# Convolution and involution in shared rounds of the array, and products in pairs (layer 1)

## The chip, the cores and the metric

The kernel runs on one core of a Trainium2 chip. The metric is the device time of one execution in microseconds. A profiled execution gives the trace, in which each engine's instructions stand with their start and length.

## What is computed

The program has two layers over 16 images of 16 channels and 256 x 256 points, all in float32. Layer 0 is a Laplace-type neural operator built on Fourier transforms; the change does not touch it. Layer 1 is this (cut to what matters; `x` is the group-normalised input, seen as B*C single-channel images):

```python
f = mish(conv2d(xs, W1, b1))                      # 1 -> 4 features, 3x3
top, bot = f[:, :, :H2], f[:, :, H2:]             # upper and lower half of the rows
ker = conv2d(relu(conv2d(bot, Wred, bred)), Wspan, bspan)   # 4 -> 1 -> 9, 1x1
patches = conv_general_dilated_patches(top, (3, 3), ...)    # 9 neighbours of each point
top_inv = (patches * ker[:, None]).sum(axis=2)    # the involution
shuffled = concatenate([ti, roll(bo, -1, axis=1)], axis=3).reshape(B, 4 * C, H, W)
out = mish(conv2d(shuffled, W2, b2))              # second convolution, 64 -> 16, 3x3
gate = sigmoid(...out.mean(axis=(2, 3))...)
return x * gate
```

Since `ker` is linear in the reduced value r with a bias per neighbour, the kernel forms the involution as (patches . Wspan) * r + (patches . bspan): two products on TensorE with fixed weights (`kernel` 0 and 1), a multiplication and an addition on VectorE.

## The kernel before

Layer 1 (function `layer1`) works in units. A unit is two places of one image, a place being 14 rows of each half and 8 of the 16 channels; an image has 9 units, so there are 144. Unit i's input `z` is loaded from the DRAM tensor `zn` two units ahead by SP's queue (`load_rows`, line 1115). Its steps on TensorE are these.

- `convolve(turn)`, line 1144, is the first convolution, half of the channel pairs in each of two turns. A product takes 18 rows of `z` (16 and the two neighbours) to 64 outputs, over 512 columns (2 channels x 256), and three products, one for each dx, add up in PSUM. The row group is given by half and place (4 groups of 32 rows), the column group by place and by `a`. So one round, dx fixed, is 8 products on 8 tiles of 32 x 64: the whole array of 128 x 128. The four PSUM banks are evacuated by Mish on ScalarE, into `bot` (line 1153) and into `feat`, which is one of the two `wide` tiles (line 1161).
- `reduce`, line 1172, makes r from `bot`: 8 products on tiles of 64 x 32, and a Relu on ScalarE. It then issues the stores of `bot` to the DRAM tensor `cf` from GpSimd's queue (line 1242).
- `involution(kernel)`, line 1194, takes 32 rows of `feat` to 32 outputs: one round, dx fixed, is 16 products on 16 tiles of 32 x 32. Its four banks `pd` are evacuated by VectorE: for kernel 0 `t = pd * r` (line 1209), for kernel 1 `top = pd + t` (line 1211). Then the eight stores of `top` to `cf` are issued (line 1224).
- The second convolution of the image before, `conv2`, runs beside the units of this one, one of its eight steps a unit. Its input `rows` comes back from `cf` (line 1250), VectorE makes four `planes` of sums and differences of it (line 1263), and TensorE forms four products (line 1272), each of 8 products of 128 x 32 on 4 tiles. VectorE and ScalarE combine them into the even and odd columns. The last image has a routine of its own, `conv2_last`.

All PSUM tiles of layer 1 come from one pool of eight banks (`bank`), which go round. The order of work on TensorE, ScalarE, VectorE and GpSimd is the order of the program (`tc.manual_schedule`), written out in the loop at the end of `layer1`. `conv2`, `gate` and `conv2_last` are generators; each `next` runs one to its next `yield`. With `nxt` the unit after `now`, TensorE's order in a usual unit is: convolve 0 of `nxt`, involution 0 of `now`, product 1, involution 1, product 2, convolve 1 of `nxt`, product 0, reduction of `nxt`, product 3. The ninth unit of an image, and all of the first image's, have no products.

Of the kernel before, what the change touches and what calls it, by code (L numbers as in the profile page):

```python
# [10 lines left out]
F32 = mybir.dt.float32  # L11
I32 = mybir.dt.int32
AF = mybir.ActivationFunctionType
ALU = mybir.AluOpType
# [5 lines left out]
N = 256  # L20
G = 8
P = 128
# [1001 lines left out]
def layer1(ctx, tc, d, zn, cf, mr, nb):  # L1024
# [17 lines left out]
    def bank(shape, name):  # L1042
        return banks.tile([P, *shape], F32, tag="bank", name=name)
# [76 lines left out]
    class Unit:  # L1120
# [3 lines left out]
        def __init__(self, b, i, n):  # L1124
            self.b, self.i = b, i
            j, h = divmod(n, 2)
            self.places = [(2 * j + s, 8 * h) for s in range(2)] if n < 8 else [(8, 0), (8, 8)]
            self.z = load_rows(b, self.places)

        def convolve(self, turn):  # L1130

            if turn == 0:
                self.bot = fp.tile([P, 8, 2, H], F32, tag="bot", name="bot")
                self.feat = wide[self.i % 2]
            ps = {(half, a): bank([2, N], "c1") for half in (1, 0) for a in range(2)}
            for dx in range(3):
                for a in range(2):
                    c = 4 * a + 2 * turn
                    for half in (1, 0):
                        for s in range(2):  # L1140
                            p = 32 * (2 * half + s)
                            lanes = slice(p, p + 18)
                            to = 64 * (s ^ a)
                            nc.tensor.matmul(  # L1144
                                ps[half, a][to : to + 64],
                                lhsT=w1[lanes, dx],
                                rhs=self.z[lanes, c : c + 2, dx : dx + N],
                                start=dx == 0,
                                stop=dx == 2,
                            )  # L1150
            for a in range(2):
                c = 4 * a + 2 * turn
                nc.scalar.activation(  # L1153
                    self.bot[:, c : c + 2],
                    ps[1, a].rearrange("p c (x e) -> p c e x", e=2)[:, :, ::-1],
                    AF.Mish,
                    bias=b1[1],
                )
            for a in range(2):
                c = 4 * a + 2 * turn  # L1160
                nc.scalar.activation(  # L1161
                    self.feat[:, c : c + 2, 1 : N + 1], ps[0, a], AF.Mish, bias=b1[0]
                )

        def reduce(self):

# [15 lines left out]
                nc.scalar.activation(self.r[:, s], ps[s], AF.Relu, bias=bred)  # L1182
            store_bot(self.b, self.places, self.bot)

        def involution(self, kernel):

            parts = [(s, fp_) for s in range(2) for fp_ in range(2)]
            ps = [bank([2, N], "pd") for _ in parts]
            for dx in range(3):
                for k in range(4):  # L1190
                    for (s, half), out in zip(parts, ps):
                        p = 64 * (s ^ k // 2) + 32 * half
                        lanes = slice(p, p + 32)
                        nc.tensor.matmul(  # L1194
                            out[32 * k : 32 * k + 32],
                            lhsT=dw[lanes, kernel, dx],
                            rhs=self.feat[lanes, 2 * k : 2 * k + 2, dx : dx + N],
                            start=dx == 0,
                            stop=dx == 2,
                        )  # L1200
            if kernel == 0:
                self.t = rp.tile([P, 2, 2, 2, 2, H], F32, tag="t", name="t", bufs=1)
                self.top = fp.tile([P, 2, 2, 2, 2, H], F32, tag="top", name="top")
            r = self.r.rearrange("p s (c q) x -> p s c q x", q=2)
            for (s, half), out in zip(parts, ps):
                out = out.rearrange("p c (x e) -> p c e x", e=2)[:, :, ::-1]
                t = self.t[:, s, half]
                if kernel == 0:
                    nc.vector.tensor_tensor(t, out, r[:, s], ALU.mult)  # L1209
                else:  # L1210
                    nc.vector.tensor_tensor(self.top[:, s, half], out, t, ALU.add)  # L1211
            if kernel:
                store_top(self.b, self.places, self.top)

    def valid(t):
        return (0 if t == 0 else 1), (16 if t == 8 else 15)
# [48 lines left out]
    def conv2(b, s, acc):  # L1265

        def products(terms):
            ps = bank([4, H], "c2ps")
            for i, (w, src) in enumerate(terms):
                for blk in range(2):  # L1270
                    for j in range(4):
                        nc.tensor.matmul(  # L1272
                            ps[32 * j : 32 * j + 32],
                            lhsT=w[:, blk],
                            rhs=src[:, 4 * j + blk : 4 * j + blk + 4],
                            start=(i, blk) == (0, 0),
                            stop=(i, blk) == (len(terms) - 1, 1),
                        )
# [12 lines left out]

        if b == nb - 1:
            yield from conv2_last(b, s, products, pooled)
            return
        a = rp.tile([P, 4, H], F32, tag="mid", name="mid", bufs=2)
        nc.scalar.copy(a, product(1))
        following(1)
        yield
        ps = product(2)
        even = rp.tile([P, 4, H], F32, tag="even", name="even", bufs=2)  # L1300
        odd = rp.tile([P, 4, H], F32, tag="odd", name="odd", bufs=2)
        yield
        nc.vector.tensor_tensor(even, ps, a, ALU.add)
        nc.vector.tensor_tensor(odd, a, ps, ALU.subtract)
        following(2)
        yield
        nc.vector.tensor_tensor(even, product(0), even, ALU.add)
        following(0)
        yield
        pooled(even, 0)  # L1310
        nc.vector.tensor_tensor(odd, odd, product(3), ALU.subtract)
        following(3)
        yield
        pooled(odd, 1)
        yield
# [80 lines left out]
    with tc.manual_schedule(engines={E.PE, E.Activation, E.DVE, E.Pool}):  # L1396
        begin_unit(0)
        begin_unit(1)
        u = units[0]
        u.convolve(0)  # L1400
        u.convolve(1)
        u.reduce()
        acc, last, first, second = None, iter(()), iter(()), iter(())
        for i in range(9 * nb + 12):
            b, s = divmod(i, 9)
            now, nxt = units.pop(i, None), units.get(i + 1)
            begin_unit(i + 2)
            if s >= 7 and b < nb:
                conv2_rows(b, s - 7)
            if b == nb and 0 < s < 7:  # L1410
                conv2_rows(b - 1, s + 1)
            if s < 6 and 0 < b < nb:
                conv2_rows(b - 1, s + 2)
            fresh = s == 8 and b < nb - 1
            gated = s == 8 and 0 < b <= nb
            next(last, None)
            if nxt:
                nxt.convolve(0)
            if s < 8 and b and b <= nb:
                if s == 0:  # L1420
                    acc = sm.tile([P, 16], F32, tag="acc", name="acc")
                second = conv2(b - 1, s, acc)
            if now:
                now.involution(0)
            next(first, None)
            next(second, None)
            if now:
                now.involution(1)
            if fresh:
                plane(b, 0, 1)  # L1430
            next(second, None)
            if gated:
                last = gate(b - 1, acc)
                next(last)
            if nxt:
                nxt.convolve(1)
            next(second, None)
            if fresh:
                plane(b, 0, 2)
            next(second, None)  # L1440
            if fresh:
                plane(b, 0, 0)
            if nxt:
                nxt.reduce()
            next(second, None)
            if gated:
                next(last)
            if fresh:
                plane(b, 0, 3)
            if gated:  # L1450
                next(last)
            next(last, None)
            first, second = second, iter(())

# [188 lines left out]
```

## Time and profile before

| | us |
|---|---|
| median of 3 runs (lowest, highest) | 5987.47 (5984.29, 5995.61) |
| profiled execution, its own time | 6010.53 |
| its span, from the first to the last instruction | 6008.8 |
| layer 1 within the span | from 2937 to 5975 |
| busy time of TensorE, VectorE, GpSimd, ScalarE over the span | 5572.9, 4666.5, 2802.4, 2310.8 |
| mean granted TensorE clock | 0.978 |

Busy times of one engine are the union of its instructions' times. The ends of matmuls are modelled, so TensorE's stages are measured from start to start. A float32 product leaves two MATMUL and two LDWEIGHTS records in the trace: 27648 records for the involution are 13824 products.

### The profile page before, as it was taken

Reading aid. Unit: us, or ns where it says so; the run is one execution under the profiler, and the core shown is the slowest. Engines: PE = TensorE matmul, PEld = TensorE weight load, DVE = VectorE, ACT = ScalarE, POOL = GpSimd, SP = SyncE. Lnnn points to the kernel's source line nnn. Section 1 sums busy time; section 2 is a strip of 40 time slices with the busy share of each in tenths; the row PEclk is TensorE's granted clock in tenths of the full one; section 3 lists DMA queues with packets and bytes.
Section 4 is the critical chain, followed back from the end, with each engine's and each line's share of the span. In section 5 each row is a group of like instructions: output and inputs, shape, how many; then the busy total and the mean of one; then the engine's idle time right before and its main releaser. Section 6 shows DMA issues by size and latency. Waiting matters only on the chain.

```text
span 6008.8 us, 216283 instructions
## 1 busy us (share of the span) xinstructions
PE 5572.9 (93%) x94280; PEld 3166.7 (53%) x94280; DVE 4666.5 (78%) x8643; ACT 2310.8 (38%) x4158; POOL 2802.4 (47%) x4090
## 2 busy tenths in 40 slices
PE   6999999688988888999899999999999999999996
PEld 5888888576766766777433333333333333333332
DVE  8888888388887876888557787777877778777784
ACT  2344556344444442222233333333333333333331
POOL 1344444333333335666544555544555445544453
PEclk9999999899999999999899999999999999999998
DMA  3455555566565658999677888888888888888886
GB/s 96 142 141 160 164 143 144 159 189 199 193 200 190 194 193 294 326 327 326 216 217 217 280 269 268 251 242 272 271 267 251 243 268 279 264 250 251 262 278 225
DMA packets 814469, 1370.07 MB, mean 228 GB/s; under 512 B 139824, under 2 KB 629168, under 8 KB 798384
## 3 DMA queue, kind: packets, MB, share of 16 engines
q1 hardware_dynamic: 596176, 881.61, 46.5%
q0 software_dynamic: 217344, 474.61, 25.8%
q8 instruction: 741, 12.14, 0.8%
q14 instruction: 208, 1.70, 0.1%
HBM read 729.78 MB, written 556.47 MB: 214 GB/s over the span
## 4 chain that ended last, share of the span: by engine, by line
PE 66%; DVE 20%; DMA 8%; issue 4%; ACT 1%; POOL 1%; SPq 1%; DVEq 0%; ACTq 0%; POOLq 0%
PE pd L1194 16%; PE c2ps L1272 15%; PE c L1144 12%; DMA z<-in_x 5%; PE ph L760 4%; PE ps L706 3%; PE pg L725 3%; PE pr L1172 2%; DVE planes L1263 2%; PE py L951 2%; PE py L952 2%; DVE st L167 2%; PE pt L741 2%; DVE zb L983 1%; DVE st L968 1%
## 5 line engine op out<-in xcount | busy, mean ns | idle before, releaser
L1224 POOL DMA_DIRECT2D cf<-top x1152 | 668.3, 692 | 1162.8 <-DVE top L1211 987.0
L1263 DVE TENSOR_TENSOR planes<-rows 128x1152 f32<-128x1152 f32 x960 | 1203.4, 1295 | 0.1
L1194 PE MATMUL pd<-wide,dw 32*32 32x512 f32 x27648 | 1032.8, 599 | 32.8 <-issue 17.6
L1153 ACT ACTIVATE bot<-c,b 128x512 f32<-128x512 f32 x576 | 364.8, 684 | 1450.9 <-PE c L1144 1099.4
L1144 PE MATMUL c<-z,w 18*64 18x512 f32 x13824 | 835.1, 601 | 15.7 <-DMA z<-zn 15.7
L1194 PEld LDWEIGHTS pd<-wide,dw 32*32 32x32 f32 x27648 | 446.6, 103 | 595.7 <-issue 455.5
L1209 DVE TENSOR_TENSOR t<-pd,r 128x512 f32<-128x512 f32 x576 | 357.5, 682 | 482.3 <-PE pd L1194 481.7
L1144 PEld LDWEIGHTS c<-z,w 18*64 18x64 f32 x13824 | 293.2, 132 | 533.4 <-issue 410.8
L1242 POOL DMA_DIRECT2D cf<-bot x720 | 395.4, 622 | 198.3 <-DMA cf<-top 81.2
L780 POOL TENSOR_TENSOR h<-w 128x256 f32<-128x256 f32 x258 | 211.4, 820 | 583.7 <-DVE w L774 580.8
L1272 PE MATMUL c2ps<-planes,c 128*32 128x512 f32 x3968 | 477.1, 598 | 0.0
L1211 DVE TENSOR_TENSOR top<-pd,t 128x512 f32<-128x512 f32 x576 | 357.4, 682 | 106.4 <-PE pd L1194 106.1
L1369 POOL TENSOR_SCALAR o<-o,scale,mean 128x258 f32<-128x258 f32 x488 | 355.5, 736 | 155.9 <-DVE scale L1361 141.5
L964 POOL TENSOR_TENSOR x<-x,o 128x512 f32<-128x512 f32 x256 | 324.5, 1268 | 215.1 <-DVE o L963 215.1
L205 PE MATMUL pu<-fy,f 128*128 128x128 f32 x2048 | 414.8, 285 | 1.1 <-ACT u L219 1.0
L212 PE MATMUL pv<-at,f 128*128 128x128 f32 x2048 | 403.1, 279 | 0.0
L322 POOL DMA_DIRECT2D al<-o x544 | 338.3, 629 | 118.1 <-ACT o L313 79.2
L1161 ACT ACTIVATE wide<-c,b 128x512 f32<-128x512 f32 x576 | 365.0, 693 | 0.0
L725 PE MATMUL pg<-alb,s 128*32 128x64 f32 x16896 | 288.0, 222 | 70.7 <-issue 52.3
L706 PE MATMUL ps<-tt,lt 64*32 64x256 f32 x8448 | 292.3, 388 | 54.0 <-issue 20.5
L951 PE MATMUL py<-h,iy 128*128 128x256 f32 x1024 | 316.4, 391 | 10.7 <-DMA h<-hd 10.7
L760 PE MATMUL ph<-ix,yt 64*128 64x128 f32 x4128 | 294.2, 281 | 31.2 <-DVE w L774 22.0
(244 smaller groups left out, 9937.8 us busy)
## 6 DMA issues: line engine op xcount, KB each, us to landing
rows<-cf SPq DMA_DIRECT2D x128, 2176.0 KB
cf<-top POOLq DMA_DIRECT2D x896, 112.0 KB, 5.5
cf<-bot POOLq DMA_DIRECT2D x336, 224.0 KB, 6.4
z<-zn SPq DMA_DIRECT2D x576, 129.0 KB
alb<-alx SPq DMA_DIRECT2D x132, 512.0 KB
zn<-zb SPq DMA_DIRECT2D x128, 516.0 KB
o<-zn SPq DMA_DIRECT2D x128, 516.0 KB
z<-in_x SPq DMA_DIRECT2D x64, 1024.0 KB
```

The source lines that it names most:

```text
L205: nc.tensor.matmul(pu[:, h, :, :, e].rearrange("p v g m -> p (v g) m"), lhsT=f[:, e, c, h], rhs=fy[:, e].rearrange("p (n m) -> p n m", m=2 ...
L212: nc.tensor.matmul(pv[:, a, h], lhsT=f[:, e, c, h], rhs=at[:, e, 4 * cg + c].rearrange("p l m -> p (l m)"), start=e == 0, stop=e == 1,)
L706: nc.tensor.matmul(ps[32 * g : 32 * g + 32, odd, v], lhsT=lt[lanes, kk, g, 1 - v : 3 - v].rearrange("p l c -> p (l c)"), rhs=tt[lanes, kk, g],
L725: nc.tensor.matmul(ps[32 * q : 32 * q + 32, x], lhsT=s[:, i].rearrange("p v k -> p (v k)"), rhs=alb[:, :, column(i)], start=True, stop=True,)
L760: nc.tensor.matmul(ph[q][:, e, blocks], lhsT=yt[lanes, i].rearrange("p t k -> p (t k)"), rhs=ix[lanes, i].rearrange("p (b x) -> p b x", b= ...
L951: nc.tensor.matmul(py[:, e], lhsT=iy[:, e], rhs=h[:, e, k % 4], start=True, stop=False)
L1144: nc.tensor.matmul(ps[half, a][to : to + 64], lhsT=w1[lanes, dx], rhs=self.z[lanes, c : c + 2, dx : dx + N], start=dx == 0, stop=dx == 2,)
L1194: nc.tensor.matmul(out[32 * k : 32 * k + 32], lhsT=dw[lanes, kernel, dx], rhs=self.feat[lanes, 2 * k : 2 * k + 2, dx : dx + N], start=dx == 0,
L1224: nc.gpsimd.dma_start(out=rows[y + 2 * lo : y + 2 * hi, :, c + 2 * k : c + 2 * k + 2].rearrange("y f c x -> y f (c x)"), in_=o[32 * k + 2 ...
L1242: nc.gpsimd.dma_start(out=rows[y + 4 * lo : y + 4 * hi, to : to + n].rearrange("p c x -> p (c x)"), in_=src.rearrange("p c q x -> p (c q x)"),
L1263: nc.vector.tensor_tensor(planes[:, k, rows], x[:, rows], y[:, rows], op_)
L1272: nc.tensor.matmul(ps[32 * j : 32 * j + 32], lhsT=w[:, blk], rhs=src[:, 4 * j + blk : 4 * j + blk + 4], start=(i, blk) == (0, 0), stop=(i, ...
```

## The change

`convolve` and `involution` no longer run as stages of their own. A new function `phases(nxt, now, turn)` takes both: for two groups y it opens two banks for the convolution and two for the involution, and for each dx it issues four convolution products (tiles of 32 x 64) and then eight involution products (tiles of 32 x 32) on the other eight sub-arrays. From y = 0 to y = 1 the two swap places. Evacuation becomes `activate` and `combine`, called after each group. A unit calls `phases` twice, with turn 0 and 1, which is also the involution's `kernel`. Two `yield`s leave `conv2` between products 1 and 2, and between 0 and 3. TensorE's order in a usual unit becomes: `phases` 0, products 1 and 2, `phases` 1, products 0 and 3, reduction. The stores of `top` are issued after `phases` 1.

The diff, without unchanged bodies:

```diff
@@ -1126,41 +1126,70 @@
...
             self.z = load_rows(b, self.places)
-
-        def convolve(self, turn):
-
-            if turn == 0:
+            self.feat = wide[i % 2]
+
+        def convolve(self, turn, banks_, dx):
+
+            for (half, a), ps in banks_.items():
+                c = 4 * a + 2 * turn
+                for s in range(2):
+                    p, to = 32 * (2 * half + s), 64 * (s ^ a)
+                    lanes = slice(p, p + 18)
+                    nc.tensor.matmul(
+                        ps[to : to + 64],
+                        lhsT=w1[lanes, dx],
+                        rhs=self.z[lanes, c : c + 2, dx : dx + N],
+                        start=dx == 0,
+                        stop=dx == 2,
+                    )
+
+        def activate(self, turn, banks_):
+
+            if turn == 0 and not hasattr(self, "bot"):
                 self.bot = fp.tile([P, 8, 2, H], F32, tag="bot", name="bot")
-                self.feat = wide[self.i % 2]
-            ps = {(half, a): bank([2, N], "c1") for half in (1, 0) for a in range(2)}
-            for dx in range(3):
-                for a in range(2):
-                    c = 4 * a + 2 * turn
-                    for half in (1, 0):
-                        for s in range(2):
-                            p = 32 * (2 * half + s)
-                            lanes = slice(p, p + 18)
-                            to = 64 * (s ^ a)
-                            nc.tensor.matmul(
-                                ps[half, a][to : to + 64],
-                                lhsT=w1[lanes, dx],
-                                rhs=self.z[lanes, c : c + 2, dx : dx + N],
-                                start=dx == 0,
-                                stop=dx == 2,
-                            )
-            for a in range(2):
+            for (half, a), ps in sorted(banks_.items(), reverse=True):
                 c = 4 * a + 2 * turn
...
-                )
+                if half:
+                    nc.scalar.activation(
+                        self.bot[:, c : c + 2],
+                        ps.rearrange("p c (x e) -> p c e x", e=2)[:, :, ::-1],
+                        AF.Mish,
+                        bias=b1[1],
+                    )
+                else:
+                    nc.scalar.activation(
+                        self.feat[:, c : c + 2, 1 : N + 1], ps, AF.Mish, bias=b1[0]
+                    )
+
+        def involution(self, kernel, banks_, dx):
+
+            for q in range(2):
+                for right in range(2):
+                    for (s, half), ps in banks_.items():
+                        k = 2 * right + q
+                        p = 64 * (s ^ right) + 32 * half
+                        lanes = slice(p, p + 32)
+                        nc.tensor.matmul(
+                            ps[32 * k : 32 * k + 32],
+                            lhsT=dw[lanes, kernel, dx],
+                            rhs=self.feat[lanes, 2 * k : 2 * k + 2, dx : dx + N],
+                            start=dx == 0,
+                            stop=dx == 2,
+                        )
+
+        def combine(self, kernel, banks_):
+
+            if kernel == 0 and not hasattr(self, "t"):
+                self.t = rp.tile([P, 2, 2, 2, 2, H], F32, tag="t", name="t", bufs=1)
+                self.top = fp.tile([P, 2, 2, 2, 2, H], F32, tag="top", name="top")
+            r = self.r.rearrange("p s (c q) x -> p s c q x", q=2)
+            for (s, half), ps in banks_.items():
+                ps = ps.rearrange("p c (x e) -> p c e x", e=2)[:, :, ::-1]
+                t = self.t[:, s, half]
+                if kernel == 0:
+                    nc.vector.tensor_tensor(t, ps, r[:, s], ALU.mult)
+                else:
+                    nc.vector.tensor_tensor(self.top[:, s, half], ps, t, ALU.add)
 
...
 
-        def involution(self, kernel):
-
-            parts = [(s, fp_) for s in range(2) for fp_ in range(2)]
-            ps = [bank([2, N], "pd") for _ in parts]
+    def phases(nxt, now, turn):
+
+        for y in range(2):
+            ours, theirs = ((0, y), (1, 1 - y)), ((1 - y, 0), (y, 1))
+            c1 = {part: bank([2, N], "c1") for part in ours if nxt}
+            pd = {part: bank([2, N], "pd") for part in theirs if now}
             for dx in range(3):
-                for k in range(4):
-                    for (s, half), out in zip(parts, ps):
-                        p = 64 * (s ^ k // 2) + 32 * half
-                        lanes = slice(p, p + 32)
-                        nc.tensor.matmul(
-                            out[32 * k : 32 * k + 32],
-                            lhsT=dw[lanes, kernel, dx],
-                            rhs=self.feat[lanes, 2 * k : 2 * k + 2, dx : dx + N],
-                            start=dx == 0,
-                            stop=dx == 2,
-                        )
...
-            if kernel:
-                store_top(self.b, self.places, self.top)
+                if nxt:
+                    nxt.convolve(turn, c1, dx)
+                if now:
+                    now.involution(turn, pd, dx)
+            if nxt:
+                nxt.activate(turn, c1)
+            if now:
+                now.combine(turn, pd)
+        if now and turn:
+            store_top(now.b, now.places, now.top)
...
@@ -1295,18 +1312,15 @@
...
         following(1)
-        yield
         ps = product(2)
         even = rp.tile([P, 4, H], F32, tag="even", name="even", bufs=2)
         odd = rp.tile([P, 4, H], F32, tag="odd", name="odd", bufs=2)
-        yield
         nc.vector.tensor_tensor(even, ps, a, ALU.add)
         nc.vector.tensor_tensor(odd, a, ps, ALU.subtract)
         following(2)
         yield
         nc.vector.tensor_tensor(even, product(0), even, ALU.add)
         following(0)
-        yield
         pooled(even, 0)
         nc.vector.tensor_tensor(odd, odd, product(3), ALU.subtract)
         following(3)
@@ -1396,14 +1410,13 @@
     with tc.manual_schedule(engines={E.PE, E.Activation, E.DVE, E.Pool}):
         begin_unit(0)
         begin_unit(1)
-        u = units[0]
-        u.convolve(0)
-        u.convolve(1)
-        u.reduce()
-        acc, last, first, second = None, iter(()), iter(()), iter(())
+        for turn in range(2):
+            phases(units[0], None, turn)
+        units[0].reduce()
+        acc, last, before = None, iter(()), iter(())
         for i in range(9 * nb + 12):
             b, s = divmod(i, 9)
-            now, nxt = units.pop(i, None), units.get(i + 1)
+            now, nxt, conv = units.pop(i, None), units.get(i + 1), iter(())
...
             fresh = s == 8 and b < nb - 1
             gated = s == 8 and 0 < b <= nb
             next(last, None)
-            if nxt:
-                nxt.convolve(0)
+            next(before, None)
+            phases(nxt, now, 0)
             if s < 8 and b and b <= nb:
                 if s == 0:
                     acc = sm.tile([P, 16], F32, tag="acc", name="acc")
-                second = conv2(b - 1, s, acc)
-            if now:
-                now.involution(0)
-            next(first, None)
-            next(second, None)
-            if now:
-                now.involution(1)
+                conv = conv2(b - 1, s, acc)
+            next(conv, None)
             if fresh:
                 plane(b, 0, 1)
-            next(second, None)
             if gated:
                 last = gate(b - 1, acc)
                 next(last)
-            if nxt:
-                nxt.convolve(1)
-            next(second, None)
             if fresh:
                 plane(b, 0, 2)
-            next(second, None)
+            phases(nxt, now, 1)
+            next(conv, None)
             if fresh:
                 plane(b, 0, 0)
             if nxt:
                 nxt.reduce()
-            next(second, None)
             if gated:
...
-            first, second = second, iter(())
+            before = conv
```

More of the change, by code (lines that the diff above doesn't have):

```diff
@@ L1128, in __init__ @@
             self.z = load_rows(b, self.places)
-        def convolve(self, turn):
-            if turn == 0:
-                self.bot = fp.tile([P, 8, 2, H], F32, tag="bot", name="bot")
-                self.feat = wide[self.i % 2]
-            ps = {(half, a): bank([2, N], "c1") for half in (1, 0) for a in range(2)}
-            for dx in range(3):
-                for a in range(2):
-                    c = 4 * a + 2 * turn
-                    for half in (1, 0):
-                        for s in range(2):
-                            p = 32 * (2 * half + s)
-                            lanes = slice(p, p + 18)
-                            to = 64 * (s ^ a)
-                            nc.tensor.matmul(
-                                ps[half, a][to : to + 64],
-                                lhsT=w1[lanes, dx],
-                                rhs=self.z[lanes, c : c + 2, dx : dx + N],
-                                start=dx == 0,
-                                stop=dx == 2,
-                            )
-            for a in range(2):
-                c = 4 * a + 2 * turn
[L1153 to L1157, printed above, removed]
-                )
[L1159 to L1162, printed above, removed]
-                )
@@ L1183, in reduce @@
             store_bot(self.b, self.places, self.bot)
-        def involution(self, kernel):
-            parts = [(s, fp_) for s in range(2) for fp_ in range(2)]
-            ps = [bank([2, N], "pd") for _ in parts]
-            for dx in range(3):
-                for k in range(4):
-                    for (s, half), out in zip(parts, ps):
-                        p = 64 * (s ^ k // 2) + 32 * half
-                        lanes = slice(p, p + 32)
-                        nc.tensor.matmul(
-                            out[32 * k : 32 * k + 32],
-                            lhsT=dw[lanes, kernel, dx],
-                            rhs=self.feat[lanes, 2 * k : 2 * k + 2, dx : dx + N],
-                            start=dx == 0,
-                            stop=dx == 2,
[L1200 to L1211, printed above, removed]
-            if kernel:
-                store_top(self.b, self.places, self.top)
+    def phases(nxt, now, turn):
[3 more added lines that the diff above has]
+            pd = {part: bank([2, N], "pd") for part in theirs if now}
+            for dx in range(3):
+                if nxt:
[8 more added lines that the diff above has]
+            store_top(now.b, now.places, now.top)
     def valid(t):
```

## Prediction

> **What bounds the kernel now.** The page is read first: where TensorE is busy, and what ended last.
>
> ```profile
> span 6008.8 us, 216283 instructions
> ...
> PE 5572.9 (93%) x94280; PEld 3166.7 (53%) x94280; DVE 4666.5 (78%) x8643; ACT 2310.8 (38%) x4158; POOL 2802.4 (47%) x4090
> ...
> PE 66%; DVE 20%; DMA 8%; issue 4%; ACT 1%; POOL 1%; SPq 1%; DVEq 0%; ACTq 0%; POOLq 0%
> PE pd L1194 16%; PE c2ps L1272 15%; PE c L1144 12%; DMA z<-in_x 5%; PE ph L760 4%; PE ps L706 3%; PE pg L725 3%; PE pr L1172 2%; DVE planes L1263 2%; PE py L951 2%; PE py L952 2%; DVE st L167 2%; PE pt L741 2%; DVE zb L983 1%; DVE st L968 1%
> ```
>
> The chain that ended last lies on TensorE, and its three longest lines (involution, second convolution, first convolution) are those that the change regroups. The second view is the stretch table, for all of layer 1 and for one unit:
>
> ```profile
> 2937.00:5975.00 3038.00, 2984.54 (x52128) 1004.29 (x52128) 2265.65 (x2941) 1137.60 (x2081) 1495.48 (x2472) 0.99 0.83 255
> ```
> ```profile
> 4499.39:4519.99 20.60, 20.60 (x372) 6.66 (x368) 17.03 (x21) 8.10 (x15) 6.75 (x12) 1.00 0.84 245
> ```
>
> After the length come PE, PEld, DVE, ACT and POOL. In the unit TensorE is busy for the whole 20.60 us, at the full clock; VectorE has 17.03. So a unit costs what TensorE's stages cost. Those are in the timeline:
>
> ```profile
> 4502.72 1.92 PE L1272 MATMUL c2ps<-planes,w_difference 128*32 128x512 f32 x16
> 4504.57 2.83 PE L1144 MATMUL c<-z,w 18*64 18x512 f32 x48
> 4507.33 1.92 PE L1272 MATMUL c2ps<-planes,c 128*32 128x512 f32 x16
> 4509.19 1.09 PE L1172 MATMUL pr<-bot,wr 64*32 64x512 f32 x16
> 4510.21 1.92 PE L1272 MATMUL c2ps<-planes,c 128*32 128x512 f32 x16
> 4512.06 2.83 PE L1144 MATMUL c<-z,w 18*64 18x512 f32 x48
> 4514.82 3.40 PE L1194 MATMUL pd<-wide,dw 32*32 32x512 f32 x96
> 4518.16 0.64 PE L1272 MATMUL c2ps<-planes,w_sum 128*32 128x512 f32 x4
> ```
>
> Start to start, a stage is: first convolution (one turn) 2.76 us, involution (one kernel) 3.34, one product of the second convolution 1.85, reduction 1.02. A float32 product leaves two records, so a pass over the tiles in use has 8 records in the first convolution (6 passes), 16 in the involution (6), 4 in a product (4), 8 in the reduction (2). Two passes cost 1.02 and four 1.85: some 0.42 a pass, and about 0.18 that each stage pays once; the records' starts give a pass as 0.427 to 0.43. **A stage's time follows its passes, not how many tiles it fills**: 4 tiles and 8 tiles give the same pass. Only with 16 tiles is it longer: 3.34 for six passes against 2.76, 0.58 lost per involution in the spacing of the starts.
>
> Where that 0.18 sits is seen where involution is followed by convolution (two short windows: 13 involution records in flight, then the products and the weight loads of the next stage):
>
> ```profile
> 3009.33 1.04 PE L1194 MATMUL pd<-wide,dw 32*32 32x512 f32 x13
> 3010.30 0.69 PE L1144 MATMUL c<-z,w 18*64 18x512 f32 x8
> ```
> ```profile
> 3010.30 0.23 PEld L1144 LDWEIGHTS c<-z,w 18*64 18x64 f32 x16 [0.84 <-DVE t L1209]
> ```
>
> In the trace the last involution product starts at 3009.78 and the first convolution product at 3010.30, 0.516 us later: a pass (0.427) and 0.09. That holds in all 23 places of this kind, and the reverse change takes 0.516 in all 143. The convolution's first tile lies on sub-arrays whose last involution products, third and seventh of the sixteen, began at least 0.17 us before the last one of all, so it was free that much sooner and was not used; nor are weights loaded ahead: PEld starts together with PE.
>
> **What the Trainium skill says.** "TensorEngine Tiling (Array Packing)", section "Key Properties": "Changing tiling mode (not just tile) drains the TensorE"; its section "Available Configurations" lists 32x64 and 32x32 as separate modes. The trace agrees: each change of shape costs a finished pass plus 0.09 us, inside one shape no such gap stands. "TensorE: Matmul & The Clock Gate", section "LDWEIGHTS (loading the stationary operand)", puts a load at its columns over 1.2 GHz, 27 ns for 32 and 53 for 64; the trace agrees (first pass 54 ns longer than the later ones in the convolution, 27 in the reduction). With 0.09 it makes up the 0.18.
>
> **The change, part by part.** Same products, same arithmetic, other order.
>
> (1) *Rounds.* Before, a unit has four such stages: 2 x 2.76 + 2 x 3.335 = 12.19 us. After, `phases` runs per turn two groups (y) of three rounds (dx); in each round four convolution products of 18x64, then eight involution products of 32x32, on the other half of the array. By what the skill states and the 23 + 143 places show, shape 32x32 does not start before shape 18x64 is through. Then each round is two stages of two passes. Convolution: load 0.053 + passes 0.854 + starts of four records 0.020 + drain 0.09 = 1.017. Involution: 0.027 + 0.854 + eight starts 0.047 + 0.09 = 1.018; the reduction, eight tiles and two passes, is measured at 1.02. A unit has 2 x 2 x 3 rounds x 2 = 24 stages: 24.46 us, **+12.27** a unit. 143 of the 144 units run paired: **+1755 us**. The gain of 0.58 in the spacing with 16 tiles is inside that figure, as stages of eight tiles do not have it.
>
> (2) *First and last.* The first convolution and the last involution run alone, half the array, one shape: 24 passes x 0.43 = 10.3 plus 0.18, against 5.52 and 6.67: **+9**.
>
> (3) *Products two and two.* Products 1, 2 stand together, and 0, 3. One stage of eight passes is 1.02 + 6 x 0.43 = 3.60 instead of 3.71: 0.11 x 2 x 120 conv2 steps (the last image has its own routine, unchanged) = **-26**.
>
> (4) *VectorE, ScalarE.* Same instructions (`t`, `top` 682 ns, Mish 690 ns) in another order. They evacuate four banks per 6.1 us group instead of four or eight in a row; eight banks turn round, so a group finds banks that were filled a group or more before. Cost nothing: TensorE hides them, 33 us a unit against VectorE's 17. If that cover were gone, the price would be VectorE's 17 against some 19 in the rival below.
>
> (5) *Stalls that go.* Layer 1 holds stages longer than their kind's usual time; summed (actual less count x usual) that is 83 + 10 in the involution, 38 in the reduction, 10 in the first convolution, 6 in the products: some 150 us, from waits for VectorE at the start of an image, for Mish before the reduction, and for `zn`. With 12 us more per unit most of the first two have time to finish: Mish of the convolution's half runs under the round's involution stage. Between 0 and -150; I take **-80**. What is late next is TensorE itself.
>
> (6) *DMAs.* The eight stores of `top` a unit (line 1224, POOL's queue) come after the second `phases` rather than before the second convolve; those of `bot` follow as before. On SP's queue the loads of `rows` and `z` keep their order. In a unit of 33 us each has more time, and the readers of `cf` are an image later. Nothing; without that cover a store is 0.7 us of POOL.
>
> Sum: 1755 + 9 - 26 - 80 = +1658. The profiled execution took 6010.5 us, 23 above the median of 5987.5, which I keep: 5987 + 1658 = **7645 us**. Each 0.01 us of error per stage is 34 us; 0.99 to 1.05 gives -100 to +100, the stalls -70 to +80: 7480 to 7820.
>
> **Rivals.** (B) *The two shapes run side by side*, because the drain is asked for only where a new tile touches one of another shape in flight; every change in the trace before does touch one. Then a group of three rounds is six passes, 2.76 us; four of them 11.04 against 12.19; x 143 = -164, with the products -190: 5795; without a drain between the two groups 0.09 x 2 less a unit, 5770. Up to 100 is taken back if VectorE, 17 of then 19 us, holds up the banks. 5750 to 5900. For it: twelve tiles are fewer than the sixteen that cost 0.58. Against it: the whole array is waited for in all 166 places, also where the tile itself was free. It decides if TensorE keeps account by tile and not for the whole array.
>
> (C) *A change of shape costs 0.09, but the passes of both overlap.* 27 stages a unit against the 7 of (B): 20 x 0.09 x 143 = +257, less 190: some 6055. Against it: no place in the trace has 0.09 without the pass ahead of it.
>
> **How the numbers follow.** The drain as reckoned 0.85, (B) 0.12, (C) 0.02, the rest near no change. About 0.2% is what a measurement of this kernel can tell. Slower: 0.85 + 0.02; faster 0.12; same 0.01. The range is the first case's, as it alone holds over 8 in 10: 7480 to 7820.
>
> **What would show it.** Right: in the timeline the first convolution comes in groups of 8 records and the involution in groups of 16, starts 1.02 us apart, alternating, 33 us between units; PE's busy share near 95%, VectorE's down to about 62%. Step 3: c2ps groups of 32 records, 3.60. Wrong: convolution products that start while involution products are in flight, groups of three rounds in 2.8 us, a TensorE unit under 20 us (B); groups 0.5 us apart (C).

## The result, and the profile after

The changed kernel takes 7577.0 us in the median (7572.9 to 7585.2), against 5987.0 on the same chip: a ratio of 1.2654, 95% interval 1.2632 to 1.2676. The forecast was 7645 within 7480 to 7820. The profiled execution of the changed kernel has a span of 7577.9 us.

The page after, its span, the engines' busy times and the chain that ended last:

```profile
span 7577.9 us, 215984 instructions
...
PE 7187.1 (95%) x94280; PEld 3120.9 (41%) x94280; DVE 4699.8 (62%) x8643; ACT 2355.3 (31%) x4158; POOL 2722.8 (36%) x4090
...
PE 76%; DVE 13%; DMA 6%; issue 2%; ACT 1%; POOL 1%; SPq 0%; DVEq 0%; ACTq 0%; POOLq 0%
PE c L1138 23%; PE pd L1172 23%; PE c2ps L1289 12%; DMA z<-in_x 4%; PE ph L760 3%; PE ps L706 3%; PE pg L725 2%; PE pr L1201 2%; PE py L951 2%; PE py L952 1%; PE pt L741 1%; DVE st L167 1%; DVE zb L983 1%; DVE st L968 1%; DVE alx L656 1%
```

As many products as before (94280 records), and VectorE, ScalarE and GpSimd are busy for nearly as many microseconds as before (within 3%). Only TensorE has grown, by 1614 us, and the two lines that now share rounds (1138 convolution, 1172 involution) went from 28% of the chain to 46% of a longer one. A 95% busy TensorE is, in the shared rounds, one that is half empty: busy says that some product is in flight, not how many tiles are.

The table by stretch, for layer 1 and for one unit (after the length: PE, PEld, DVE, ACT, POOL, clock, DMA share, GB/s):

```profile
2931.00:7544.00 4613.00, 4596.88 (x52128) 953.95 (x52128) 2298.03 (x2941) 1182.11 (x2081) 1418.26 (x2472) 1.00 0.59 168
```
```profile
5410.12:5442.73 32.61, 32.61 (x380) 6.71 (x372) 11.31 (x16) 8.42 (x15) 9.70 (x19) 1.00 0.54 151
```

A unit is 32.61 us now instead of 20.60, with the same products (the edges of the window take in 8 records more), and TensorE is never idle in it. The timeline shows what fills it (start, length, engine, line, records):

```profile
5409.10 1.09 PE L1201 MATMUL pr<-bot,wr 64*32 64x512 f32 x16
5410.12 1.09 PE L1138 MATMUL c<-z,w 18*64 18x512 f32 x8
5411.14 1.09 PE L1172 MATMUL pd<-wide,dw 32*32 32x512 f32 x16
5412.15 1.09 PE L1138 MATMUL c<-z,w 18*64 18x512 f32 x8
5413.17 1.09 PE L1172 MATMUL pd<-wide,dw 32*32 32x512 f32 x16
...
5420.29 1.09 PE L1138 MATMUL c<-z,w 18*64 18x512 f32 x8
5421.31 1.09 PE L1172 MATMUL pd<-wide,dw 32*32 32x512 f32 x16
5422.33 1.92 PE L1289 MATMUL c2ps<-planes,w_sum 128*32 128x512 f32 x16
5424.07 1.90 PE L1289 MATMUL c2ps<-planes,w_difference 128*32 128x512 f32 x16
5425.90 1.09 PE L1138 MATMUL c<-z,w 18*64 18x512 f32 x8
```

The columns to read are start and records. Eight convolution records, then sixteen of the involution, strictly in turn, each stage 1.02 us from start to start, whether it fills four tiles or eight. Over the whole trace the median stage is 1.018 us (1716 of the convolution and 1716 of the involution, all between 1.017 and 1.020), and at all 3169 changes between the two shapes the first product of one starts 0.516 or 0.517 us after the last of the other. The weight loads of a stage start with its products:

```profile
5412.15 0.21 PEld L1138 LDWEIGHTS c<-z,w 18*64 18x64 f32 x8 [0.84 <-issue]
5413.17 0.18 PEld L1172 LDWEIGHTS pd<-wide,dw 32*32 32x32 f32 x16 [0.81 <-issue]
```

### The profile page after: what moved, and what is told of

Read it like the earlier page. It is cut to its first block, busy times and chain, and to the rows that moved or that the text cites. A ratio compares the mean times of both kernels' runs of the same rounds, so it can differ in the third digit from the quotient of the medians.

```text
span 7577.9 us, 215984 instructions
## 1 busy us (share of the span) xinstructions
PE 7187.1 (95%) x94280; PEld 3120.9 (41%) x94280; DVE 4699.8 (62%) x8643; ACT 2355.3 (31%) x4158; POOL 2722.8 (36%) x4090
## 3 DMA queue, kind: packets, MB, share of 16 engines
q0 software_dynamic: 217344, 474.61, 21.3%
## 4 chain that ended last, share of the span: by engine, by line
PE 76%; DVE 13%; DMA 6%; issue 2%; ACT 1%; POOL 1%; SPq 0%; DVEq 0%; ACTq 0%; POOLq 0%
PE c L1138 23%; PE pd L1172 23%; PE c2ps L1289 12%; DMA z<-in_x 4%; PE ph L760 3%; PE ps L706 3%; PE pg L725 2%; PE pr L1201 2%; PE py L951 2%; PE py L952 1%; PE pt L741 1%; DVE st L167 1%; DVE zb L983 1%; DVE st L968 1%; DVE alx L656 1%
## 5 line engine op out<-in xcount | busy, mean ns | idle before, releaser
L1138 PE MATMUL c<-z,w 18*64 18x512 f32 x13824 | 1880.6, 616 | 20.1 <-DMA z<-zn 20.1
L1172 PE MATMUL pd<-wide,dw 32*32 32x512 f32 x27648 | 1875.8, 599 | 0.0
L1153 ACT ACTIVATE bot<-c,b 128x512 f32<-128x512 f32 x576 | 395.9, 687 | 2697.4 <-PE c L1138 2238.0
L1138 PEld LDWEIGHTS c<-z,w 18*64 18x64 f32 x13824 | 361.7, 130 | 1452.4 <-issue 1303.9
L1172 PEld LDWEIGHTS pd<-wide,dw 32*32 32x32 f32 x27648 | 312.3, 103 | 1396.4 <-issue 1041.7
L1289 PE MATMUL c2ps<-planes,c 128*32 128x512 f32 x3968 | 452.2, 595 | 2.1 <-DVE planes L1334 2.1
L1160 ACT ACTIVATE wide<-c,b 128x512 f32<-128x512 f32 x576 | 391.8, 680 | 0.0
L760 PE MATMUL ph<-ix,yt 64*128 64x128 f32 x4128 | 296.7, 282 | 31.1 <-DVE w L774 22.9
L205 PEld LDWEIGHTS pu<-fy,f 128*128 128x128 f32 x2048 | 319.8, 197 | 1.1
```

Source lines behind the costliest of these rows:

```text
L205: nc.tensor.matmul(pu[:, h, :, :, e].rearrange("p v g m -> p (v g) m"), lhsT=f[:, e, c, h], rhs=fy[:, e].rearrange("p (n m) -> p n m", m=2 ...
L760: nc.tensor.matmul(ph[q][:, e, blocks], lhsT=yt[lanes, i].rearrange("p t k -> p (t k)"), rhs=ix[lanes, i].rearrange("p (b x) -> p b x", b= ...
L1138: nc.tensor.matmul(ps[to : to + 64], lhsT=w1[lanes, dx], rhs=self.z[lanes, c : c + 2, dx : dx + N], start=dx == 0, stop=dx == 2,)
L1172: nc.tensor.matmul(ps[32 * k : 32 * k + 32], lhsT=dw[lanes, kernel, dx], rhs=self.feat[lanes, 2 * k : 2 * k + 2, dx : dx + N], start=dx == ...
L1289: nc.tensor.matmul(ps[32 * j : 32 * j + 32], lhsT=w[:, blk], rhs=src[:, 4 * j + blk : 4 * j + blk + 4], start=(i, blk) == (0, 0), stop=(i, ...
```

## The experiments

Each was compared with the kernel before on the same chip; the ratios below are to that kernel.

### One shape in the shared rounds (e1_one_shape)

Edit, to the changed kernel:

```diff
-                    nc.tensor.matmul(
-                        ps[to : to + 64],
-                        lhsT=w1[lanes, dx],
+                    for g in range(0, 64, 32):
+                        nc.tensor.matmul(
+                            ps[to + g : to + g + 32],
+                            lhsT=w1[lanes, dx, g : g + 32],
...
```

> The order of the changed kernel, but each convolution product of 64 outputs becomes two of 32, so that all tiles of a group are 32x32. Theory (a change of shape waits for the whole array): no wait is left within a group, a group of three rounds is 96 records on 16 tiles as the involution was before, and the two groups of a call follow without a change: 6.53 us a call instead of 12.2. Per paired unit 13.06 instead of 24.43, x 143 = -1627 us: 5950 to 6050. Rival (the interleaving itself halves the array: order of issue or banks, not the shape): no gain, 7570 or more, as there are more products.

Measured 6196.1 us, 1.0348 (1.0331 to 1.0365). With 13824 more records it is 1381 us faster than the changed kernel. Timeline, start of a call of `phases`:

```profile
4487.33 1.12 PE L1139 MATMUL c<-z,w 18*32 18x512 f32 x12
4487.86 0.66 PE L1173 MATMUL pd<-wide,dw 32*32 32x512 f32 x8
4488.22 0.67 PE L1139 MATMUL c<-z,w 18*32 18x512 f32 x5
4488.31 0.64 PE L1173 MATMUL pd<-wide,dw 32*32 32x512 f32 x8
4488.41 1.14 PE L1139 MATMUL c<-z,w 18*32 18x512 f32 x11
```

Involution products begin while convolution products are in flight; 18 rows beside 32 did not keep them apart. The least time of a call is 6.530 us, as expected, and an undisturbed unit 21.3 us. So the shape, and neither order nor banks, is what halves the array. The total lies some 150 us above the upper end of what was expected, because the mean call takes 7.38 us; that is taken up below.

### The shapes apart within a group (e2_shapes_apart)

```diff
             for dx in range(3):
                 if nxt:
                     nxt.convolve(turn, c1, dx)
+            for dx in range(3):
                 if now:
```

> In each group of the changed kernel the three rounds of the convolution come first and then the three of the involution: same products, same banks, same half of the array for each; 8 stages a unit instead of 24. Theory: a stage is its load, 6 passes of 0.427 and 0.09, so 2.73 us; 8 x 2.73 = 21.84 against 24.43 a unit, x 143 = -370: about 7205. The half-filled array then accounts for some 9.6 us a unit of the added 12.2, the changes of shape for 2.6. Rival (shapes overlap, only a fixed price per change): 16 changes a unit fewer and overlap as before, under 6100.

Measured 7205.4 us, 1.2036 (1.2015 to 1.2056). Timeline:

```profile
5405.87 2.80 PE L1138 MATMUL c<-z,w 18*64 18x512 f32 x24
5408.60 2.81 PE L1172 MATMUL pd<-wide,dw 32*32 32x512 f32 x48
5411.34 2.81 PE L1138 MATMUL c<-z,w 18*64 18x512 f32 x24
5414.07 2.81 PE L1172 MATMUL pd<-wide,dw 32*32 32x512 f32 x48
```

Stages of six passes start 2.73 or 2.74 us apart. This splits the loss: 372 us of the changed kernel's 1590 come from changing shape after every round, not after every third; the rest is still there, as each stage of six passes fills half the array. Making the changes rarer did not make half-filled stages cheap.

### Products two and two alone (e3_pairs_only)

In the kernel before, three `yield`s of `conv2` left out (the changed kernel leaves out the same three) and the calls of `next` placed as in the changed kernel:

```diff
         following(1)
-        yield
         ps = product(2)
...
-        yield
         nc.vector.tensor_tensor(even, ps, a, ALU.add)
...
         following(0)
-        yield
         pooled(even, 0)
```

> The kernel before with only the products two and two: products 1 and 2 after involution 0, products 0 and 3 after the second convolve, each pair in one stage. Theory: 0.138 us saved a pair (3.571 against 2 x 1.854), x 240 = -33 us: about 5955. Rival (VectorE's bursts of 6.4 us then hold banks or planes up): up to 40 us of new stalls, 5990 or more.

Measured 5972.5 us, 0.9969 (0.9958 to 0.998). An undisturbed unit fell from 20.6 to 20.4 us, the first unit of an image rose from 24.1 to 26.5 and the ninth fell from 14.9 to 13.1. The saving of an undisturbed unit is of the expected size; net, -19 us by the ratio came of the expected -33. Both theories hold a part.

### Stages grouped by shape (e4_grouped)

The order of the kernel before rewritten. `conv2` issues its products 1, 2, 0, 3 in one step, then `even` and `odd`, then the four planes; a unit is

```diff
                 nxt.convolve(0)
+                nxt.convolve(1)
...
                 now.involution(0)
+                now.involution(1)
...
             next(second, None)
...
                 nxt.reduce()
```

> The kernel before with its stages grouped by shape: both convolves, both involutions, all four products, reduction; VectorE combines the four products before it forms the next planes. Theory: 4 stages a unit instead of 9: 5.33 + 6.53 + 7.0 + 1.02 = 19.88 against 20.6, x 120 = -86, and -5 in the units without products: about 5895. Rival (eight banks do not cover longer stages; Mish and VectorE hold them): the gain is eaten, 5960 or more, with waits of the involution or the products for VectorE.

Measured 5985.7 us, 0.9994 (0.9981 to 1.0008): nothing gained. Timeline:

```profile
4503.76 5.41 PE L1144 MATMUL c<-z,w 18*64 18x512 f32 x96
4509.09 6.60 PE L1194 MATMUL pd<-wide,dw 32*32 32x512 f32 x192
4515.62 1.92 PE L1272 MATMUL c2ps<-planes,w_sum 128*32 128x512 f32 x16
...
4522.63 1.09 PE L1172 MATMUL pr<-bot,wr 64*32 64x512 f32 x16
4523.65 1.93 PE L1144 MATMUL c<-z,w 18*64 18x512 f32 x26
```

Unit to unit 19.89 us, as reckoned: fewer changes of shape give just what their price says. But the first unit of an image took 29 to 33 us instead of 24, and that alone ate some 7 us per image, as much as the seven units after it (5) and the ninth (2) had saved. In each of these fourteen first units TensorE's granted clock fell to half for 10 to 17 us. One of them, and the unit after it (PE, PEld, DVE, ACT, POOL, then the clock):

```profile
4745.51:4775.03 29.52, 27.82 (x372) 11.67 (x371) 21.91 (x43) 6.69 (x11) 19.00 (x33) 0.77 0.69 213
4775.03:4795.32 20.29, 20.29 (x372) 7.93 (x368) 17.66 (x20) 8.09 (x15) 18.65 (x19) 1.00 0.77 258
```

Over layer 1's units the clock was at half for 188 us, all in fourteen first units, against 24 us in the kernel before. At half speed that is about 94 us of lost work, an estimate, or 6.7 us an image, and so nearly the whole loss. Each stretch begins within 7 us of TensorE's wait for the gate's `totals` (23.4 us in 13 waits); that this pause brings the clock down was not tried.

### Planes formed ahead (e5_planes_ahead, e6_grouped_ahead, e10_pairs_ahead)

```diff
             if s < 7:
                 plane(b, s + 1, k)
+            elif b + 1 < nb - 1:
+                plane(b + 1, 0, k)
...
-            if s >= 7 and b < nb:
-                conv2_rows(b, s - 7)
+            early = 6 if 0 < b < nb - 1 else 7
+            if b < nb and s in (early, 8):
+                conv2_rows(b, int(s == 8))
...
-            fresh = s == 8 and b < nb - 1
+            fresh = s == 8 and b == 0 and nb > 1
```

> The kernel before, where the planes for an image's first step of the second convolution are formed in the unit of the last step of the image before, each after the product that frees its plane, and not all in the ninth unit (their rows are loaded one unit sooner). Theory: what makes the first unit of an image 24.1 us instead of 20.6, and the ninth 14.9 instead of 13.1, is VectorE with 10 us of planes in a short unit; these stalls are those that the changed kernel lost. About 14 x 5.3 = -74 us: 5915. Rival (they come from the gate or from the loads of rows): within 20 us of the kernel before.

Applied to the kernel before: 5955.1 us, 0.9936 (0.9913 to 0.9959), a little under half of the expected gain. The first unit of an image came down from 24.1 to 20.5 us in most images. The ninth stayed at 14.9 to 17.7: that part of the expectation failed.

> The grouped kernel (four stages a unit) with the planes formed ahead in the same way. Theory: its undisturbed unit is 19.9 us, and the first unit of an image took 31 only because VectorE still had the planes of the ninth to form; with these gone an image takes some 176 us instead of 188: x 14 = -155, so 5830, below both kernels. Rival (four-stage grouping needs more banks than there are): no change against the grouped kernel, 5985.

Applied to the grouped kernel: 5931.2 us, 0.9901 (0.9885 to 0.9918), faster than the kernel before and than the grouped one, though only about a third of what was expected: the first unit of an image still took 23 to 29 us. The trace shows the clock again: it was at half for 10 to 14 us in ten of fourteen first units, which took 27.4 to 29.1 us, and two units without such a stretch took 22.9 and 24.4. In all 143 us of the units ran at half, some 72 us of lost work, by the same estimate, of the 101 that were missing. Why the clock falls there is open.

> Products two and two, with the planes of the next image's first step formed ahead, in the kernel before; its convolve and involution stages as they are. Theory: the two gains add, -0.3% and -0.6%: 0.991, about 5935, as the grouped version with planes ahead. Rival (bursts of VectorE in pairs cost what the planes gave): 0.996.

Applied to the pairs: 5955.9 us, 0.9921 (0.9896 to 0.9946). The sum of the two gains (0.9905) lies within the interval, but so does the gain of the planes alone (0.9936): whether they add is not shown. The rival's 0.996 lies outside.

### Easing VectorE in the one-shape kernel (e7_one_shape_eased)

The planes formed ahead as above, and:

```diff
         nc.scalar.copy(a, product(1))
-        following(1)
         ps = product(2)
...
         nc.vector.tensor_tensor(odd, a, ps, ALU.subtract)
+        following(1)
         following(2)
...
         nc.vector.tensor_tensor(even, product(0), even, ALU.add)
-        following(0)
         pooled(even, 0)
         nc.vector.tensor_tensor(odd, odd, product(3), ALU.subtract)
+        following(0)
         following(3)
```

> The kernel with all tiles 32x32 in shared rounds, with the planes formed ahead, and VectorE combining each pair of products before it forms planes. Theory: that kernel's undisturbed unit is 21.3 us; the units of 22 to 29 us between are VectorE's order of work. An image of 8 x 21.3 + 13.9 = 184 us instead of 199 would give -210: 5990 to 6080, still not below the kernel before, as 16 tiles take 3.3 us for three rounds. Rival (the stalls are TensorE's own, from more products): 6150 or more.

Measured 6242.6 us, 1.0423 (1.0403 to 1.0442): no better than the one-shape kernel, somewhat worse. The theory fell; easing VectorE's order of work in this way did not shorten the units of 22 to 29 us. A new one came from the traces. Two of TensorE's waits in the one-shape kernel, in total, times, longest:

```profile
PE pd L1173 <- issue: 49.7, 39, 3.9
PE c L1139 <- issue: 30.4, 26, 3.4
```

These products wait for nothing that the profile shows. One of the gaps in the timeline:

```profile
3017.57 1.37 PE L1139 MATMUL c<-z,w 18*32 18x512 f32 x15
...
3020.54 0.18 PEld L1173 LDWEIGHTS pd<-wide,dw 32*32 32x32 f32 x16 [2.51 <-issue]
3020.54 1.09 PE L1173 MATMUL pd<-wide,dw 32*32 32x512 f32 x16 [1.60 <-issue]
```

Loads and products stand still together, the products for 1.6 us, and neither waits for a semaphore. The page's DMA queues have one that brings instructions, before and one-shape:

```profile
q8 instruction: 741, 12.14, 0.8%
```
```profile
q8 instruction: 848, 13.89, 0.9%
```

12.14 MB over 94280 x 2 load and product records is 64 bytes a record, and the added 1.75 MB fits 13824 x 2 more, so this queue carries TensorE's program, 16 KB or 256 instructions a packet. In the eased kernel's trace all 82 gaps over 1 us with no semaphore to wait for ended 1.07 to 1.83 us after such a packet had landed, though packets come 6.2 us apart on average in layer 1.

### Less other traffic (e9_one_shape_less_dma)

```diff
     def conv2_rows(b, s):
+        if 8 * b + s > 1:
+            return
         t = rows2[(8 * b + s) % 2]
```

> The kernel with all tiles 32x32 in shared rounds, which reads the rows of the second convolution from DRAM for its first two steps only and uses these again after that (so the second convolution works on old data): 126 of 128 loads of 2.2 MB are left out, 274 MB of traffic. Its trace had 104 gaps over 0.7 us before products that wait for no semaphore, 110 us in all, and in the eased version such gaps ended 1.1 to 1.8 us after a packet of the queue that brings TensorE's instructions. Theory (TensorE runs out of instructions, whose packets share the 16 DMA engines): fewer such gaps, 6196 falls to some 6080 to 6140. Rival (the supply's own pace or the decoder is the limit, whatever else is moved): the gaps stay, 6170 or more.

Measured 6083.2 us, 1.0147 (1.0124 to 1.0171), 113 us below the one-shape kernel, at a DMA share of 0.58 instead of 0.82 in the same stretch. From start to start of TensorE's products, the gaps over 0.7 us without a semaphore fell from 104 (110 us beyond a pass each) to 48 (56 us), those with one nearly stayed (30 and 26). That fits instruction packets which wait among other transfers. The packets themselves took about as long (median 1.06 and 1.03 us), so such a wait would lie before they start. That the traffic itself, and not another effect of the missing loads, made the difference was not tried in a second way; the granted clock, too, was at half for 41 us of the units in the one-shape kernel and for 20 here.

### The order within sixteen tiles (e8_row_by_row)

```diff
-                for k in range(4):
-                    for (s, half), out in zip(parts, ps):
+                for (s, half), out in zip(parts, ps):
+                    for k in range(4):
```

> The kernel before, with the sixteen involution products of a round issued row group by row group (part outside, k inside) instead of column by column. It asks where 3.34 us instead of 2.76 for six passes on 16 tiles comes from. Theory (a floor per load and product pair of about 33 ns: 16 of them need 0.53 a pass): the order does not matter, 5989 within 15 us. Rival (loads of one column group, or of one row group, hold each other up): up to 0.58 x 288 = -167 us, or longer.

Measured 5981.3 us, 0.9986 (0.9975 to 0.9996), and the undisturbed unit is 20.6 us as before. Whether the sixteen products go column group by column group or bank by bank (two products of one row group, then two of another), six passes on 16 tiles take 3.3 us. That speaks for a limit on the rate of load and product pairs (0.53 us a pass for 16 pairs, 33 ns each on average) and against conflicts within a row or column group. It is no floor of each single pair: in the first pass of a stage most starts are 6 to 7 ns apart. Other orders were not tried.

## Why the prediction was right

**Which wait ends last.** The forecast took TensorE's stages as the unit's whole length and a change of shape as a wait for the whole array, also where the tiles do not touch. Both held. Before, every change touched tiles in flight, and rival (B) rested on that. In the changed kernel the tiles of a round are apart, and the interval is the same 0.516 us. The one-shape kernel then took the wait away by the shape alone. (B) and (C) are out for this placing of the tiles. In every round, though, both shapes use all four row groups and all four column groups; whether two shapes would run side by side on separate ones was not tried. What the Trainium skill says in "TensorEngine Tiling (Array Packing)", section "Key Properties", of a drain at a change of mode holds here for tiles that do not meet as well.

**The sum, term by term**, from layer 1's parts of the two traces (3038 us before, from 2937.1 to 5975.1; 4612.5 after, from 2931.5 to 7544.0):

| term | forecast | measured |
|---|---|---|
| (1) rounds, 143 paired units | +1755 | 24 x 1.018 against 12.19: +1751 |
| (2) first and last alone | +9 | last involution 8.6, not the 10.5 reckoned; the first convolution is mixed with a wait for `z` |
| (3) products two and two | -26 | 3.571 against 2 x 1.854, x 240: -33 |
| (5) stalls that go | -80 (0 to -150) | 145 down to under 3: -143 |
| sum, layer 1 | +1658 | +1574.5 |

In (1) the forecast's own parts give 12 x 1.017 + 12 x 1.018 = 24.42 us a unit, not 24.46; the slip is worth 6 us. The table is of the two profiled executions, and the one before ran 23 us above its median. By the medians (+1590) the stalls that went come to some 128 us, if (1) and (3) are as in the table.

**The mis-sized term is (5).** I took about half of the stalls to go; nearly all went, so the time fell at the lower side of the range, 68 us under the forecast. In the changed kernel the first unit of an image takes 32.9 us against 32.6 in the others, and the ninth has its undisturbed 25.4. Term (5) named the start of an image, where VectorE is late, and Mish before the reduction: the planes formed ahead show the first, since they took 24.1 us down to 20.5 in the kernel before. The stalls from TensorE's instructions I had not named at all. Where six passes take 3.3 us with 192 instructions the kernel before has 13 gaps of over 1 us without a semaphore, all before involution products, some 19 us in all beyond a pass each; the changed kernel, which takes in the same instructions half as fast, has none in its units. Nor did I name the clock: the kernel before had it at half for 24 us in its units, some 12 us of lost work, the changed kernel never.

**VectorE, ScalarE and DMAs at nothing (4, 6)** held: VectorE's 17 us lie within 32.6, and no wait of TensorE for VectorE is left in the shared rounds. (4) set the price for a lost cover at VectorE's 17 us a unit; in the one-shape kernel, at 21.3 us, TensorE's gaps without a semaphore (110 us) cost more than those with one (27 us).

**The 0.58 of sixteen tiles.** The forecast had it vanish inside the new stages; it did (1.018 for eight tiles). In one shape for both kinds a round has sixteen tiles again, and the loss came back: 6.53 us for the twelve passes of a call.

## What to carry to other kernels

Before sharing the array between two kinds of products, compare their shapes of tile: disjoint tiles ran side by side here only within one shape, and each change of shape cost a finished pass and 0.09 us, so fewer changes (372 us in the changed kernel) and stages that fill the array are what counted here. Count a stage by its passes, from start to start, and not by its busy time: half-empty stages read as 95% busy. Grouping stages of one shape gave just the price of the changes saved, and all of it was lost again at the seams (here the start of an image), where TensorE's clock fell to half; so look at the granted clock by stretch before you blame the order of work.

## What the runs showed of the hardware that I had not expected

- TensorE probably ran out of instructions at times. At 64 bytes a record and sixteen tiles in use it takes 256 instructions in some 4.3 us, and in the eased one-shape kernel gaps of 1 to 5 us stood before products with nothing to wait for, each ending 1.1 to 1.8 us after a 16 KB packet of the instruction queue. That is a part of why the mean call of the one-shape kernel took 7.38 us where the least was 6.53: over 286 calls some 240 us, of which such gaps make up 110.
- With sixteen tiles a load and product pair takes 33 ns on average in both orders that were tried. At that rate eight pairs need some 0.27 us, an estimate, which a pass of 0.427 us hides.
- The wait at a change of shape was the same whether or not the tiles touch: 0.516 or 0.517 us in both kernels.
- A short pause of TensorE at the start of an image was followed by 10 to 17 us at half the clock in the grouped kernel. The average nearly hides it: over the whole execution the clock reads 0.966 there and 0.978 before.
